# A planned mixture-of-experts kernel: TensorE's order taken from two lines instead of one

## The chip, the core and the metric

The kernel runs on one core of a Trainium2 chip. The core has a matrix engine (TensorE, PE in the profile), three engines for elementwise work (VectorE or DVE, ScalarE or ACT, GpSimd or POOL), a queue engine (SyncE or SP) and 16 DMA engines. SBUF is its working memory, PSUM the memory in eight banks that the matmuls write to. The metric is the device time of one execution in microseconds.

## What is computed

Sixteen sequences x of 256 tokens with 256 features pass through eight experts and one shared expert. All are gated feed-forward layers of width 1024, in float32:

```
g, u    = x @ Wg[e], x @ Wu[e]                  # e = 0..7, and Sg, Su
expert  = sum over e of p[b, e] * (silu(g) * u) @ Wd[e]
shared  = (silu(x @ Sg) * (x @ Su)) @ Sd
out     = x + (1 - s[b]) * expert + s[b] * shared
```

p and s are given for each sequence. The nine layers are treated alike: a coefficient made of p and s scales each hidden block.

## The kernel before, in words

The work is cut into 72 units: nine experts, two halves of the width, four groups of four sequences. Nearly every product of matrices is done in blocks with fewer multiplications than the plain way, at the price of sums of blocks.

For each unit, `unit_up` (line 622) makes the hidden blocks h. A *diagonal* step (`diagonal`, line 547) multiplies a plain block into bank D (two matmuls, the P part), ScalarE copies it out to pq, two more matmuls add the Q part to the same bank, and VectorE subtracts. There are four such steps, and only one bank D, so a step waits until the one before is consumed. An *off-diagonal* step (`offdiagonal`, line 590) does one matmul into a bank M (two of them). VectorE then adds M and a block s, which GpSimd made of pq, into a bank X (three of them): this add is called the seed. A pair of matmuls adds to that X. There are twelve such steps a unit. The results in D and X are consumed by ScalarE (silu, tile sg) for the gate half and by VectorE (multiplied by coefficient and sg, tile h) for the other half.

`unit_down` (line 709) multiplies h by Wd. VectorE and GpSimd first form four sums of blocks of h (the function `sum_`: three on VectorE, one on GpSimd, for each of two f). Then come seven products into banks dn (two of them), each of two matmuls with 512 columns. ScalarE copies a bank out to ev, and GpSimd starts a DMA that adds ev to running totals in DRAM. The down products of a unit are mixed into the up products of the next.

At the start, x is transposed on TensorE into banks dn (`make_raw`, line 447, and `make_xd`, line 409), and blocks of x and their sums are made (xd, xp), used, and kept in DRAM; later units load them. Unit 0 multiplies plain blocks. At the end, `finish` (line 819) loads the totals of a group, combines them on VectorE and GpSimd, transposes them on TensorE into banks dn and adds x. The last unit does without banks dn for its own product: `last_down` (line 884) writes it in eight steps of four matmuls to banks X and M.

What sets the order: all this is only entered into a list of operations (class `Plan`), each with an engine, a cost in us, a rank (the due place, 12 to a unit), what it depends on and the tiles it takes. `Plan.run` (line 77) then plays the list through on a clock of its own: each free engine takes the ready operation of lowest rank whose tiles are free, an operation's result can be used by another engine 0.25 us after its end (`HOP`), and transfers pass one after the other. The order in which operations are taken is the order in which the program's instructions are emitted. So every engine's order is fixed when the program is built; on the chip an engine runs it as written and waits by semaphores where an input is late.

The plan's costs are those of lines 222 to 233:

```
MM = 0.433                                    # matmul, 256 columns
TR = 0.16                                     # transpose
dve(n, stt) = (0.2 if stt else 0.12) + n * 0.00112
act(n) = 0.13 + n * 0.0009
pool(n) = 0.3 + n * 0.00215
```

The sums of h are charged 1.5 times `dve`. Tiles of one tag (banks dn, for one) are given out in the order of rank, whichever engine asks (`turn`).

TensorE is the exception to "lowest ready rank". Its operations stand in one list sorted by rank (`line`), and only the head of that list may be taken; if the head is not ready or its bank not free, TensorE waits in the plan.

Of the kernel before, what the change touches and what calls it, by code (L numbers as in the profile page):

```python
# [47 lines left out]
class Plan:  # L48
# [6 lines left out]

    HOP = 0.25
    KB = 0.0035

# [7 lines left out]
    def add(self, engine, length, rank, emit, deps=(), new=(), uses=(), lag=None, kb=None):  # L68
        lag = self.HOP if lag is None else lag
        op = Op(engine, length, lag, rank, emit, deps, list(new), list(uses))  # L70
        for b in [*op.new, *op.uses]:
            b.users += 1
        op.kb = kb
        self.ops.append(op)
        return op

    def run(self):
        free = self.slots
        ready = {}
        serial = {id(op): n for n, op in enumerate(self.ops)}  # L80
        for op in self.ops:
            ready.setdefault(op.engine, [])
        at = {id(op): 0.0 for op in self.ops}
        idle = {e: 0.0 for e in ready}
        events = []
        for op in self.ops:
            if not op.missing:
                heapq.heappush(events, (0.0, serial[id(op)], 0, op))
        order = []
        left = len(self.ops)  # L90
        line = sorted((op.rank, serial[id(op)]) for op in self.ops if op.engine == "PE")
        at_line = 0
        turn = {tag: deque() for tag in free}
        for op in sorted(self.ops, key=lambda op: (op.rank, serial[id(op)])):
            for b in op.new:
                turn[b.tag].append(b)
        now = passed = 0.0
        while left:
            while events and events[0][0] <= now + 1e-9:
                _, _, kind, op = heapq.heappop(events)  # L100
                if kind == 0:
                    heapq.heappush(ready[op.engine], (op.rank, serial[id(op)], op))
                elif kind == 1:
                    for b in [*op.new, *op.uses]:
                        b.users -= 1
                        if not b.users:
                            free[b.tag].append(b.tile)
            for e in ready:
                if idle[e] > now + 1e-9 or not ready[e]:
                    continue  # L110
                held, took = [], None
                while ready[e]:
                    item = heapq.heappop(ready[e])
                    if e == "PE" and item[:2] != line[at_line]:
                        held.append(item)
                        break
                    if all(free[b.tag] and turn[b.tag][0] is b for b in item[2].new) and all(
                        b.tile is not None for b in item[2].uses
                    ):
                        took = item[2]  # L120
                        for b in took.new:
                            b.tile = free[b.tag].popleft()
                            turn[b.tag].popleft()
                        break
                    held.append(item)
                for item in held:
                    heapq.heappush(ready[e], item)
                if took is None:
                    continue
                at_line += e == "PE"  # L130
                end = now + took.length
                idle[e] = end
                if took.kb:
                    passed = max(passed, end) + took.kb * self.KB
                    took.lag += passed - end
                order.append(took)
                left -= 1
                heapq.heappush(events, (end, serial[id(took)], 2, took))
                heapq.heappush(events, (end + took.lag, serial[id(took)], 1, took))
                for a in took.after:  # L140
                    a.missing -= 1
                    t = end if a.engine == e == "PE" else end + took.lag
                    at[id(a)] = max(at[id(a)], t)
                    if not a.missing:
                        heapq.heappush(events, (at[id(a)], serial[id(a)], 0, a))
            if left:
                if not events:
                    raise RuntimeError("the plan has come to a stop")
                now = max(now, events[0][0])
        return order  # L150
# [3 lines left out]
def kernel(  # L154
# [97 lines left out]
    def make_coef():  # L252
# [6 lines left out]
        )  # L259

    coef_op = add("DVE", 0.8, -2, make_coef)


# [5 lines left out]
    def load(rank, dst, src, kb, deps=(), new=(), uses=(), late=0, engine="SP"):  # L269
        queue = {"SP": nc.sync, "ACT": nc.scalar}[engine]  # L270
        return add(
            engine, 0.5, rank, lambda: queue.dma_start(dst(), src), deps, new, uses, lag=2.2 + late, kb=kb
        )

    def tt(engine, rank, o, a, b, op, n, deps, new=(), uses=(), slow=1.0):
        eng, length = (nc.vector, dve(n) * slow) if engine == "DVE" else (nc.gpsimd, pool(n))
        return add(engine, length, rank, lambda: eng.tensor_tensor(o(), a(), b(), op), deps, new, uses)  # L277
# [741 lines left out]
```

## Time and profile before

| | |
|---|---|
| time, median of 3 runs | 2534.58 us (2534.41 to 2534.78) |
| the profiled execution's own time | 2535.56 us |
| its span, first to last instruction | 2533.8 us |
| granted TensorE clock | 0.999 |
| HBM traffic | 167 GB/s over the span |

The profile is of one execution. Times are in us; a row of a group ends in the mean time of one instruction in ns. L277 and L282 are helpers of VectorE and GpSimd, L541 the one of all matmuls, so the tiles' names tell the operations apart: X<-M,s is the seed, h<-h,h a sum of h, dn<-h,wd a down product, dn<-ident a transpose, X<-xp,wp the pair of an off-diagonal step. A float32 matmul leaves two records. In an answer in the order of time, the first column is the start in the span, the second the time from the first start to the last end of the merged instructions, and a bracket at the end tells how long the engine was idle before and what released it. A wait is given as: engine and tile that waited, what it waited for, us in all, times, longest.

### The profile page before, as it was taken

The numbers are of one execution on the slowest core, as the hardware profiler recorded it, in microseconds if no ns is written. First come the engines' busy times: TensorE is split into PE (matmuls) and PEld (weight loads), VectorE is DVE, ScalarE is ACT, GpSimd is POOL, SyncE is SP. The second block draws the span as 40 slices with busy tenths as digits, with TensorE's granted clock in tenths as the row PEclk, the third lists the DMA queues.
The fourth block names the chain that finished last, engine by engine and source line by source line (L and its number), as shares of the span: only waits on it lengthen the run. The fifth ranks groups of instructions, "written<-read, shape, count | busy, mean of one in ns | idle before, by whom it ended". The sixth has DMA issues, their size and how long they took to land. (4 is left out here: it accounts for less than half of the span.)

```text
span 2533.8 us, 30307 instructions
## 1 busy us (share of the span) xinstructions
PE 2513.3 (99%) x9637; PEld 1817.8 (72%) x9637; DVE 1866.6 (74%) x3246; ACT 789.0 (31%) x1389; POOL 1722.7 (68%) x1652
## 2 busy tenths in 40 slices
PE   8999999999999999999999999999999999999998
PEld 5767777777777777777777777777777777777776
DVE  6796767677776768676767767677867777776687
ACT  3323333333333333333333332333332333333321
POOL 7686767676675767676766667586767676676664
PEclk9999999999999999999999999999999999999999
DMA  7545666665666566666666666566666565666566
GB/s 256 178 159 152 171 167 167 158 170 159 174 166 165 152 166 163 167 169 159 171 157 168 166 168 161 163 160 159 170 160 176 156 167 157 173 160 160 154 189 198
DMA packets 179667, 425.18 MB, mean 168 GB/s; under 512 B 15121, under 2 KB 84257, under 8 KB 170545
## 3 DMA queue, kind: packets, MB, share of 16 engines
q1 hardware_dynamic: 158224, 294.18, 34.8%
q0 software_dynamic: 20224, 128.53, 27.5%
q8 instruction: 76, 1.25, 0.2%
q14 instruction: 87, 0.70, 0.1%
q10 hardware_dynamic: 1056, 0.52, 0.1%
HBM read 276.90 MB, written 146.28 MB: 167 GB/s over the span
## 5 line engine op out<-in xcount | busy, mean ns | idle before, releaser
L277 POOL TENSOR_TENSOR s<-pq,pq 128x512 f32<-128x512 f32 x852 | 1145.3, 1373 | 495.8 <-DVE X L277 476.1
L541 PE MATMUL dn<-h,wd 128*128 128x512 f32 x1988 | 1015.1, 592 | 0.0
L541 PE MATMUL X<-xp,wp 128*128 128x256 f32 x3408 | 875.3, 379 | 6.1 <-DVE X L277 6.0
L277 DVE TENSOR_TENSOR X<-M,s 128x512 f32<-128x512 f32 x852 | 589.4, 694 | 392.3 <-PE M L541 255.5
L541 PEld LDWEIGHTS X<-xp,wp 128*128 128x128 f32 x3408 | 646.6, 190 | 218.2 <-issue 107.1
L541 PE MATMUL D<-xd,wb 128*128 128x256 f32 x2272 | 583.7, 379 | 2.7 <-ACT sg L639 2.2
L541 PEld LDWEIGHTS M<-xp,wp 128*128 128x128 f32 x1704 | 323.3, 190 | 347.1 <-issue 335.3
L282 DVE SCALAR_TENSOR_TENSOR h<-X,coef,sg 128x256 f32<-128x256 f32 x852 | 393.7, 479 | 211.4 <-PE X L541 158.9
L541 PE MATMUL M<-xp,wp 128*128 128x256 f32 x1704 | 506.9, 379 | 0.5 <-DVE X L277 0.5
L761 ACT COPY ev<-dn 128x512 f32<-128x512 f32 x490 | 287.8, 587 | 681.1 <-PE dn L541 681.1
L541 PEld LDWEIGHTS D<-xd,wb 128*128 128x128 f32 x2272 | 431.0, 190 | 66.2 <-ACT sg L639 4.6
L277 DVE TENSOR_TENSOR h<-h,h 128x512 f32<-128x512 f32 x426 | 453.5, 1090 | 0.0
L541 PEld LDWEIGHTS dn<-h,wd 128*128 128x128 f32 x1988 | 377.4, 190 | 51.2
L568 ACT COPY pq<-D 128x512 f32<-128x512 f32 x284 | 166.5, 586 | 418.1 <-PE D L541 389.2
L639 ACT ACTIVATE sg<-X 128x512 f32<-128x512 f32 x434 | 258.4, 595 | 111.9 <-PE X L541 104.6
L776 POOL DMA_DIRECT2D total<-ev x132 | 116.6, 884 | 208.2 <-ACT ev L761 199.3
L277 DVE TENSOR_TENSOR pq<-D,pq 128x256 f32<-128x256 f32 x568 | 222.5, 416 | 29.5 <-PE D L541 29.3
L639 ACT ACTIVATE sg<-D 128x512 f32<-128x512 f32 x142 | 84.8, 597 | 483.5 <-DVE pq L277 483.5
L277 POOL TENSOR_TENSOR h<-h,h 128x512 f32<-128x512 f32 x142 | 199.5, 1405 | 49.3 <-PE dn L541 31.0
L277 POOL TENSOR_TENSOR wp<-wb 128x128 f32<-128x128 f32 x216 | 139.4, 681 | 0.0
L282 DVE SCALAR_TENSOR_TENSOR h<-D,coef,sg 128x256 f32<-128x256 f32 x284 | 134.9, 475 | 0.0
L282 DVE SCALAR_TENSOR_TENSOR wp<-wb,wp 128x256 f32<-128x256 f32 x102 | 89.9, 882 | 0.0
(73 smaller groups left out, 482.6 us busy)
## 6 DMA issues: line engine op xcount, KB each, us to landing
xp<-keep_p SPq DMA_DIRECT2D x408, 384.0 KB, 4.0
total<-ev POOLq DMA_DIRECT2D x70, 1024.0 KB, 7.9
xd<-keep_d SPq DMA_DIRECT2D x136, 512.0 KB, 3.5
total<-ev POOLq DMA_DIRECT2D x70, 768.0 KB, 6.8
wb<-in_L_cond_Wg_dram SPq DMA_DIRECT2D x32, 256.0 KB, 5.2
wb<-in_L_cond_Wu_dram SPq DMA_DIRECT2D x32, 256.0 KB, 5.2
wd<-in_L_cond_Wd_dram SPq DMA_DIRECT2D x64, 128.0 KB, 4.0
keep_p<-xp SPq DMA_DIRECT2D x18, 384.0 KB, 4.0
```

Of the source, the lines that this page charges most:

```text
L277: return add(engine, length, rank, lambda: eng.tensor_tensor(o(), a(), b(), op), deps, new, uses)
L282: lambda: nc.vector.scalar_tensor_tensor(o(), a(), c() if callable(c) else c, b(), ALU.mult, op),
L541: lambda: nc.tensor.matmul(o(), w(), mv(), start=start, stop=stop, skip_group_check=onto),
L568: lambda: nc.scalar.copy(p_[:, 2 - 2 * a : 4 - 2 * a, :], bank[:, :, :]), ps,
L639: lambda: nc.scalar.activation(b[:, :, :], bank[:, :, :], AF.Silu), deps, [b], [bank],
L761: lambda ev=ev, at=at, bank=bank: nc.scalar.copy(ev[:, at, :], bank.tile.rearrange("p a t -> p (a t)")),
L776: nc.gpsimd.dma_start(total[g][part], ev[:, 0:k, :], accum_op=ALU.add)
```

## The change

Each TensorE operation gets a stream: 1 if it takes or uses a tile with the tag dn (down products and all transposes), 0 otherwise (everything in banks D, M and X, the last unit's down product among them). Each stream has its own list sorted by rank. TensorE, when free in the plan, goes through its ready operations by rank; one that isn't the head of its own list is set aside and the search goes on, where before it ended. It takes the first head whose tiles are free. So a down product may pass a waiting up product, or the other way, while the order within each list stays as it was.

```diff
@@ add
         op.kb = kb
+        op.stream = None
+        if engine == "PE":
+            op.stream = int("dn" in [b.tag for b in [*op.new, *op.uses]])
         self.ops.append(op)
@@ run
-        line = sorted((op.rank, serial[id(op)]) for op in self.ops if op.engine == "PE")
-        at_line = 0
+        lines = {k: deque(sorted((op.rank, serial[id(op)]) for op in self.ops if op.stream == k)) for k in (0, 1)}
...
-                    if e == "PE" and item[:2] != line[at_line]:
+                    if e == "PE" and item[:2] != lines[item[2].stream][0]:
                         held.append(item)
-                        break
+                        continue
...
-                at_line += e == "PE"
+                if e == "PE":
+                    lines[took.stream].popleft()
```

## Prediction

> **What bounds the kernel now.** I read the totals of the page first, then the stages, then what TensorE (PE) waits for, then single places in the order of time.
>
> ```profile
> span 2533.8 us, 30307 instructions
> ...
> PE 2513.3 (99%) x9637; PEld 1817.8 (72%) x9637; DVE 1866.6 (74%) x3246; ACT 789.0 (31%) x1389; POOL 1722.7 (68%) x1652
> ```
>
> PE is busy all but 20.5 us; no other engine is near that. The busy time by stages shows where those 20.5 us lie (first column the stage, then its length, then each engine's busy time):
>
> ```profile
> 0.00:60.00 60.00, 53.51 (x180) 29.87 (x181) 38.66 (x74) 21.39 (x46) 44.82 (x66) 0.97 0.82 264
> 60.00:200.00 140.00, 134.91 (x520) 96.40 (x519) 120.63 (x200) 44.82 (x83) 100.60 (x101) 1.00 0.47 167
> 200.00:2400.00 2200.00, 2199.78 (x8426) 1600.38 (x8425) 1604.04 (x2803) 695.89 (x1214) 1503.91 (x1428) 1.00 0.63 164
> 2400.00:2500.00 100.00, 98.25 (x390) 70.54 (x389) 80.98 (x136) 25.72 (x45) 67.58 (x54) 1.00 0.77 221
> 2500.00:2534.00 34.00, 26.81 (x128) 20.57 (x126) 22.26 (x36) 1.20 (x2) 5.82 (x5) 1.00 0.33 109
> ```
>
> In 2200 us in the middle PE is idle for 0.22 us. An order of PE's instructions can't save anything there; it can only lose. Idle are 6.5 us up to 60 us, 5.1 up to 200, 1.8 from 2400 to 2500 and 7.2 after that, the last 3.4 of them after PE's work, when the last add and store run out. What ended PE's waits:
>
> ```profile
> PE X L541 <- DVE X L277: 6.0, 7, 1.4
> PE dn L862 <- DVE xd L277: 2.9, 3, 1.9
> PE D L541 <- ACT sg L639: 2.2, 3, 1.0
> ```
>
> So the largest item is a pair of X matmuls (the other line, in the new words) that waits for VectorE's seed of its bank, the next a transpose (the down line) that waits for a dn bank. In both cases the head of PE's one queue waits, and behind it stands work of the other kind. That is what the change is aimed at.
>
> **The change, part by part.** It adds and removes no instruction: the same 9637 matmuls, copies and DMAs. It alters the order in which the plan emits PE's instructions, and, as a consequence of times in the plan, the order on DVE, ACT, POOL and SP (the transfers of these queues go with them).
>
> *Ceiling of the gain.* The idle marked in the order of time, where the other line had work, is 0.70 us before the transposes at 96.26, before X pairs 1.36 (138.19), 1.27 (168.55), 0.62 (175.47), 1.00 (182.76), 1.01 (2430.67), 0.55 (2488.41) and 0.19 (2491.89), before transposes at the end 1.88 (2515.25), 0.70 (2517.47) and 0.35 (2524.11): 9.6 us. In the first 60 us the D pairs wait 0.92, 0.50 and 1.02 us and an M matmul 0.55; the down line holds only transposes there (0.44 us for four records), the last of them already done at 36.4, so I count 0.4 for the first wait and nothing for the others. The ceiling is 10.0 us. A down product takes 0.86 us from start to start, so one or two fill each gap. Time filled early is kept, since PE is full afterwards and DVE (1604 of 2200 us) is not; at the end the next thing late is the load of x for the last adds, which held DVE for 0.4 us up to 2525.6, 4.8 us before the last add ends at 2530.4. It doesn't take back more than that.
>
> The Trainium skill (Perfetto Trace Analysis, Identifying the Most-Contended Engine) says that the matmul row's occupancy is no measure of the distance to PE's limit. I therefore also added up start-to-start distances over the normal ones (0.43 us for 256 columns, 0.86 for 512, two records each): they exceed them by 22.2 us in all, 6.4 of it after 2400. Against 20.5 by busy time the ceiling would be some 1 us higher, and the middle stays full. The reading stands.
>
> *How much of it the plan can take.* "Ready" is decided when the program is written, by the plan's own clock; on the chip PE still runs one fixed order. A wait is filled only if the plan also sees it. The plan charges DVE 0.12 + 512 x 0.00112 = 0.69 us for an add of 512 columns, 1.5 times that (1.04) for a sum of h. Now look at two of the gaps:
>
> ```profile
> 161.94 3.26 DVE L277 TENSOR_TENSOR h<-h,h 128x512 f32<-128x512 f32 x1
> ```
>
> ```profile
> 166.25 1.02 PE L541 MATMUL dn<-h,wd 128*128 128x512 f32 x2
> ...
> 167.81 0.68 DVE L277 TENSOR_TENSOR X<-M,s 128x512 f32<-128x512 f32 x1
> ...
> 168.41 0.68 DVE L277 TENSOR_TENSOR h<-h,h 128x512 f32<-128x512 f32 x1
> 168.55 0.70 PE L541 MATMUL X<-xp,wp 128*128 128x256 f32 x2 [1.27 <-DVE X L277]
> ```
>
> ```profile
> 2512.95 1.63 DVE L277 TENSOR_TENSOR ev<-ev 128x512 f32<-128x512 f32 x1
> ...
> 2514.51 0.68 DVE L277 TENSOR_TENSOR xd<-dn,xd 128x512 f32<-128x512 f32 x1
> ...
> 2515.25 0.66 PE L862 MATMUL dn<-ident,wb 128*128 128x128 f32 x4 [1.88 <-DVE xd L277]
> ```
>
> The same form of sum takes 0.68 us in one place and 3.26 in another; that one is 2.2 us over the plan's 1.04, more than the 1.27 us wait that follows. Before 2515.25, three adds on DVE took 1.44, 1.43 and 1.63 us where the plan has 0.69: 2.4 us over, more than the 1.88. By the same count, a sum of 2.12 before 96.26 is 1.1 over (wait 0.70), an xp sum of 3.51 instead of 0.41 precedes 138.19 with no pause of DVE in between (3.1 over, wait 1.36), two sums of 3.04 together precede 175.47 (1.0 over, wait 0.62), and adds of 1.58 and 1.70 precede 2430.67 (1.9 over, wait 1.01). In these, 6.8 of the 9.6 us, DVE in the plan is early enough that PE doesn't wait there, and nothing is swapped. The waits at 2488 and 2491 have no such cause (two sums of 1.89 against 2.08 planned), those at 182.76, 2517.47 and 2524.11 only in part.
>
> Here the skill speaks against the change. SBUF — State Buffer, Who interferes with whom: a DVE instruction with two inputs in SBUF and a GpSimd instruction that reads SBUF exclude each other, and the later one waits for the whole of the other. The groups agree in kind: the seed has one input in PSUM, the sum of h two in SBUF, at equal size:
>
> ```profile
> L277 DVE TENSOR_TENSOR X<-M,s 128x512 f32<-128x512 f32 x852 | 589.4, 694 | 392.3 <-PE M L541 255.5
> ...
> L277 DVE TENSOR_TENSOR h<-h,h 128x512 f32<-128x512 f32 x426 | 453.5, 1090 | 0.0
> ```
>
> By the mean row (1090 ns) the plan's 1.04 is right and its clock ought to see most gaps: up to 10.0 us gained. By the rule, the length of a sum depends on what POOL happens to do, the gaps come from single long ones, and a plan with a mean can't see them: 0 to 3.2 us (10.0 less 6.8). The single rows, 0.68 and 3.26, side with the rule. I take half of it, 1.6 us.
>
> *What can be lost.* Where the plan sees a wait that the chip doesn't have, a down product of 0.86 us passes an X or D pair. From 200 to 2400 us I took, for all 766 X pairs, the time from the seed's end to the pair's start: median 2.8 us, smallest 0.32; where PE really waited it is 0.05. Passing one is therefore free nearly everywhere: the pair starts 0.86 later, PE has worked meanwhile, and DVE has 27% idle to absorb it. In 14 places, one for each change of weights (138 us apart), it is only 0.32 to 0.36; the plan adds 0.25 for the hand-over, so its own margin is about 0.1 us and a swap there is possible. Below nothing: a swap of work that is ready on the chip costs 0. Above: the advanced product's sum of h is late on the chip, 2.12 - 1.04 = 1.1 us. I take 0, since the margin is positive in every one of them. DVE's and POOL's order shifts a little with the plan; that moves single collisions either way, which I set at ±2 us.
>
> **Rivals.**
> - *All gaps filled* (chance 0.12): the plan is late enough in the same places. 2534.6 - 9 = 2525.6. For it: the waits are the right kind, head of line with other work behind. Against: DVE's long sums.
> - *The fixed order gains a wait in the middle* (0.07), slower than before: at each of the 17 changes of weights the plan lets a down product pass and its sum is late on the chip. 17 x 0.5 (half of 1.1) = 8.5 us: 2543.1. It decides from 0.3 us a change on. For it: margins of 0.1 us, sums of up to 3.26. Against: no such wait now, and PE needs that product late enough that most sums are long done.
> - *The plan never differs* (0.11): PE's head is always ready on the plan's clock, the program is the same, 2534.6.
>
> **How the numbers follow.** The profiled execution took 2535.56 us, its span is 2533.8; what is taken off the span is taken off the time, and I set it against the median of 2534.58, 0.98 lower. Likeliest (0.70): 2534.6 - 1.6 = 2533.0, own range 2529.5 to 2537. A measurement can tell 0.2%, 5.1 us: faster means under 2529.5, slower over 2539.6. Faster: the first rival and a tail of the likeliest, 0.12 + 0.03. Slower: 0.07. The range takes in the likeliest case, the unchanged program and the near part of both others: 2528 to 2538.5, some 0.17 left out.
>
> **What would show it.** Right: PE idle of about 19 us instead of 20.5; the 1.27 before an X pair near 168 and the 1.88 near 2515 still there in kind; from 200 to 2400 still under 1 us. Wrong: these waits gone, with down products in their places (first rival), or waits of PE on dn with DVE h or POOL h as releaser in the middle (second). If PE's order is the same throughout, the third. My weakest step is that I infer the plan's waits from its costs and the trace's durations.

## The result, and the profile after

2527.62 us (median of 9 runs) against 2534.58: 7.0 us less, ratio 0.9973 with a 95% interval of 0.9963 to 0.9983. The prediction was 2533.0, within 0.2% of no change, in a range of 2528 to 2538.5. The time lies just under the range, between the likeliest case and the rival that I had given 0.12 (all gaps filled, 2525.6), 2.0 us from that rival.

The page's head for the changed kernel, beside 2513.3 us of PE in a span of 2533.8 before:

```profile
span 2525.9 us, 30304 instructions
...
PE 2512.4 (99%) x9637; PEld 1817.6 (72%) x9637; DVE 1850.4 (73%) x3246; ACT 788.1 (31%) x1389; POOL 1718.6 (68%) x1652
```

The number of matmuls is the same, and so, nearly, is their busy time. What went is idle time. The stages of the changed kernel (stage, length, busy time of PE, PEld, DVE, ACT, POOL):

```profile
0.00:60.00 60.00, 56.62 (x194) 32.47 (x195) 41.09 (x76) 22.08 (x48) 46.25 (x68) 1.00 0.83 271
60.00:200.00 140.00, 137.27 (x530) 98.18 (x529) 127.10 (x205) 44.88 (x83) 104.94 (x104) 1.00 0.50 174
200.00:2400.00 2200.00, 2199.80 (x8425) 1600.33 (x8424) 1582.79 (x2806) 696.00 (x1215) 1497.01 (x1427) 1.00 0.63 164
2400.00:2500.00 100.00, 98.45 (x388) 70.16 (x387) 82.25 (x136) 24.55 (x43) 65.36 (x53) 1.00 0.73 211
2500.00:2534.00 34.00, 20.31 (x106) 16.52 (x104) 17.23 (x27) 0.60 (x1) 5.07 (x4) 0.97 0.33 109
```

Read the first two columns and take PE's busy time off the length: up to 60 us PE idles for 3.4 us in place of 6.5; from 60 to 200 for 2.7 in place of 5.1; in the middle for 0.2 as before; from 2400 to 2500 for 1.55 in place of 1.75; and from 2500 to the end of the span (2525.9) for 5.6 in place of 7.0 (the stage of before ends at 2533.8, so 7.0 and not the 7.2 of the prediction). So the gain lies in the first 200 us and at the end. The two profiled executions differ by 7.9 us, the medians by 7.0. Part of the rest is in the first 15 us, where the order of PE is the same in both: the execution of before had a granted clock of 0.89 there, this one 1.00, and its first transposes waited 1.64 us for x against 0.29.

PE's waits, X pairs on the seed first (6.0 us before), then transposes on a dn bank (2.9), then D (2.2):

```profile
PE X L545 <- DVE X L281: 3.5, 7, 0.7
PE dn L866 <- DVE xd L281: 1.7, 2, 1.4
...
PE D L545 <- ACT sg L643: 0.8, 2, 0.6
...
PE dn L545 <- DVE ev L281: 0.4, 1, 0.4
```

The last row is new: a down product that now stands ahead of an X pair waits at 2485.66 for the add on VectorE that empties its bank. It is not the mechanism of the slower rival, a product whose sum of h is late; no wait of that kind is on the list. In the order of time (start, length, PE's instructions), this is what shortened waits look like:

```profile
27.07 1.04 PE L427 MATMUL dn<-ident,h 128*128 128x128 f32 x8
28.70 1.13 PE L545 MATMUL D<-xd,wb 128*128 128x256 f32 x4 [0.59 <-ACT sg L643]
...
34.84 1.88 PE L545 MATMUL X<-pq,wb 128*128 128x512 f32 x4
36.56 1.02 PE L545 MATMUL dn<-h,wd 128*128 128x512 f32 x2
37.42 1.03 PE L545 MATMUL D<-xd,wb 128*128 128x256 f32 x4
```

At 27.07 eight records of transposes stand before the D that waits (0.59 us, 0.92 before); before the change they came after it, at 30.39 and 32.54. At 36.56 stands the first down product of unit 0, which before ran at 56.57, and the D behind it, which waited 0.50 us at 38.82, doesn't wait any more. Of the 2116 records of the down line, 160 stand earlier against the other line than before, and 24 later. The later ones are two matmuls of down products and one block's transposes in the first 100 us, and transposes at the end.

### The profile page after: what moved, and what is told of

Read it like the earlier page. It is cut to its first block, busy times and chain, and to the rows that moved or that the text cites. A ratio compares the mean times of both kernels' runs of the same rounds, so it can differ in the third digit from the quotient of the medians.

```text
span 2525.9 us, 30304 instructions
## 1 busy us (share of the span) xinstructions
PE 2512.4 (99%) x9637; PEld 1817.6 (72%) x9637; DVE 1850.4 (73%) x3246; ACT 788.1 (31%) x1389; POOL 1718.6 (68%) x1652
## 5 line engine op out<-in xcount | busy, mean ns | idle before, releaser
L281 POOL TENSOR_TENSOR wp<-wp,wb 128x256 f32<-128x256 f32 x108 | 81.8, 764 | 1.3
```

## The experiments

The times of before beside them are those of the same chip, 2534.75 to 2534.83 us.

**Where in the run the gain arises.** Three kernels allow passing only in a part of the run. The condition is on the rank of the lower of the two heads, `low`:

```diff
+                    if e == "PE" and item[:2] != (low := min(q[0] for q in lines.values() if q)) and not (low[0] < 60):
+                        held.append(item)
+                        continue
```

with `60 <= low[0] < 830` and `low[0] >= 830` in the two others.

> One list as before, except while the lower of the two heads has a rank under 60 (about the first 190 us): there the two lists. My theory (the plan's own clock has PE waiting in the first units where the chip waits, and ready work of the other list fills it): PE idle up to 200 us falls from 11.6 to about 6, the rest stays as before; 2529.3 us, 5.3 of the 7.0. Rival 1 (the gain comes from the 40 or so places in the middle that were also swapped, through fewer collisions of DVE and POOL): 2534 us. Rival 2 (much of the gain is in the first 15 us, a matter of chance between executions): 2532 to 2533 us.

Measured: 2529.56 us, ratio 0.9979 (0.9971 to 0.9987), 5.3 us less. PE's idle from 60 to 200 us is 2.76 us, from 15 to 60 us 0.52 in place of 2.99. Up to 200 us that makes 7.2 us in place of 11.6, not the 6 that I expected, since 3.9 of it lie in the first 15 us of the profiled execution, where nothing was reordered. The time is as my theory had it; the rivals fall.

> Two lists only while the lower head's rank is from 60 to 830 (about 190 to 2420 us), one list else. My theory: PE has no idle time there (0.22 us in 2200), so the swaps cost and bring nothing: 2534.6 us within 0.4. Rival 1: 2529 us or less. The rival of the prediction (a swapped down product that is late on the chip at a change of weights): 2537 us or more, with PE waiting on dn products.

Measured: 2534.67 us, ratio 1.0 (0.9992 to 1.0008). In this kernel 49 down products stand one X pair earlier, and its row for the middle is

```profile
200.00:2400.00 2200.00, 2199.79 (x8425) 1600.40 (x8424) 1583.63 (x2803) 695.80 (x1214) 1501.07 (x1428) 1.00 0.62 164
```

DVE is busy for 20 us less than before (1583.6 against 1604.0) and it buys nothing: PE is full either way. PE waits for 0.2 us there in all, so the slower rival of the prediction falls as well.

> Two lists only from rank 830 on (the last 110 us). My theory: the up products that pass the waiting transposes at the end, and down products that pass X pairs at 2430 and 2488, give 1.6 us: 2533.0. Rival: the end is set by the last loads, adds and stores, and nothing comes of it: 2534.6.

Measured: 2532.69 us, ratio 0.9991 (0.9983 to 0.9999), 2.1 us less, 0.5 more than expected. The three parts add up to 7.6 us against 7.0 for the whole.

**Which line passes.** Both lists, but in the condition above `item[2].stream == 1` in place of the rank: only down products and transposes may pass.

> Two lists, but only the list with down products and transposes may pass; a waiting down product or transpose holds up the others as before. My theory: nearly all of the gain in the first 200 us is of this direction (of the places there one, the transposes at 96 us with 0.70 of idle, is of the other), and the end, where up products pass transposes, is lost again: 2529.8 us. Rival (the gain needs both directions, since one line's lead must be given back by the other): 2532 us or more.

Measured: 2530.5 us, ratio 0.9983 (0.9976 to 0.999), 4.3 us less: 0.7 us short of my number, and 1.5 from the rival's. Idle after 2500 us is 6.95 us, as before the change: without up products passing transposes the end gains nothing. From 60 to 200 us it is 3.47 in place of 2.73, the wait at 96 us.

**How much comes from the first 55 us.** The condition with `low[0] < 13`.

> Two lists only while the lower head's rank is under 13 (about the first 55 us), one list after. In the prediction I counted 0.4 us for these, since I took the down list to hold nothing but transposes there. My theory now: a transpose at 27 us and the first down product of unit 0 at 36 us fill two waits, and the waits of D at 46 and of M at 54 shrink since all before them is earlier; idle from 15 to 60 us falls from 3.0 to under 1.2, and the time to 2532.6. Rival (the fall of idle in that stage needs the swaps after rank 13 too): 2534 us.

Measured: 2532.47 us, ratio 0.999 (0.9984 to 0.9997), 2.3 us less. Idle from 15 to 60 us falls from 2.99 to 0.74 us, all the rest stays (5.09 us from 60 to 200). One wait of 0.71 us is left in that stage, the M matmul's; it was 0.55 before and did not shrink as I had expected.

**What makes the plan see a wait.** Which waits are filled depends on the plan's clock, and that on its costs. First lower costs, with one list as the control and with two:

```diff
-    HOP = 0.25
+    HOP = 0.05
...
                     deps, [out_] if new else [], [x_, y_] if new else [x_, y_] if out_ in (x_, y_) else [x_, y_, out_],
-                    1.5,
+                    1.0,
```

> One list as before, with lower costs in the plan: hand-over 0.05 us in place of 0.25 and sums of h at 0.69 in place of 1.04. PE's order can't change by it; only DVE, ACT, POOL and SP are ordered otherwise. A control for the next run: 2534.6 within 2 us by every theory.

Measured: 2532.68 us, ratio 0.9991 (0.9983 to 0.9999): 2.1 us less with PE in the same order, by the order of the other engines alone.

> Two lists with the same low costs. With these the plan's clock has PE waiting in the first 60 us, hardly at all from 60 to 200 us, and for about 1 us at the end. My theory (only a wait that the plan sees is filled, and the plan sees those from 60 to 200 us because it charges 0.25 for a hand-over and 1.04 for every sum of h): the waits from 60 to 200 us, 5 us before and 2.7 after, stay as they are in the control, and the gain over the control is 3 to 4 us instead of 7. Rival (the costs don't matter, any list scheduling that is free to pass finds these places): 6 us or more over the control.

Measured: 2529.59 us, ratio 0.998 (0.9973 to 0.9988), 3.1 us under its control in place of 7.0. From 60 to 200 us the stage row is

```profile
60.00:200.00 140.00, 137.32 (x531) 98.27 (x530) 117.58 (x203) 45.51 (x84) 107.35 (x107) 1.00 0.51 177
```

which is 2.7 us idle against 3.7 in the control: 1.0 us gained there, where the old costs gain 2.4. "Stay as they are" was too strong; that lower costs halve the gain held. Then only the hand-over lowered:

> Two lists, only the plan's hand-over lowered from 0.25 to 0.05 us, what the chip shows; sums of h keep 1.04. My theory: part of the loss of the run with low costs is from this, part from the sums; this one lies between the two lists with low costs (2529.6) and with the old ones (2527.6): 2528.5. Rival (the sums alone decide which waits the plan sees): 2527.6.

Measured: 2526.16 us, ratio 0.9965 (0.9952 to 0.9977). Both expectations miss: it is 1.5 us better than with the old costs, and idle from 60 to 200 us is 1.2 us. So it is not the generous hand-over that makes the plan see the waits. Between this kernel and the one with low costs only the charge for sums of h differs, 1.04 against 0.69, and 3.4 us of time. A control with one list and only the short hand-over was not run, so how much of these differences comes from the order of the other engines is not known.

Then higher costs, again with the control. Three kinds of DVE instructions with both inputs in SBUF get about what the trace shows:

```diff
-                op = stt(rank + 1, r, x_, float(t), r, ALU.add, P, [u, v], uses=[b])
+                op = stt(rank + 1, r, x_, float(t), r, ALU.add, P, [u, v], uses=[b], more=0.6)
...
-            [bi, bj], [buf] if new else [], src if new else [buf, *src],
+            [bi, bj], [buf] if new else [], src if new else [buf, *src], 2.3,
...
-                uses=list({id(m[q][1]): m[q][1] for q in (o, a, c)}.values()),
+                uses=list({id(m[q][1]): m[q][1] for q in (o, a, c)}.values()), slow=1.5,
```

> One list, with the costs of three kinds of DVE instructions with both inputs in SBUF raised to what the trace shows: sums of x 0.94 in place of 0.41, combinations at the end 1.04 in place of 0.69, the base sum of weights 0.94 in place of 0.34. PE's order is unchanged. A control: 2534.6 within 2 us.

Measured: 2535.09 us, ratio 1.0 (0.9992 to 1.0008): by the order of the other engines alone these costs bring nothing.

> Two lists with these high costs, so that the plan sees more of the chip's waits (some 6 us from 60 to 200 us and 7 at the end in place of 3.6 and 4). My theory: 1 to 3 us less than the two lists with the old costs, 2525 to 2526.5. Rival (what is left are single long instructions of DVE that no mean cost can place): 2527.6 within 0.7.

Measured: 2522.14 us, ratio 0.995 (0.9938 to 0.9963): 12.7 us less than before, 13.0 under its control and 5.5 under the change itself, more than I expected. The stages:

```profile
0.00:60.00 60.00, 56.73 (x197) 32.74 (x198) 41.94 (x78) 22.32 (x49) 46.98 (x68) 1.00 0.83 271
60.00:200.00 140.00, 139.56 (x541) 100.71 (x540) 126.43 (x207) 46.44 (x86) 106.06 (x106) 1.00 0.50 177
...
2500.00:2534.00 34.00, 16.53 (x92) 14.15 (x90) 12.55 (x22) 0.00 (x0) 2.54 (x2) 0.94 0.33 109
```

From 60 to 200 us PE idles for 0.44 us; the control, with the same costs and one list, for 5.45. The rival, that single long instructions can't be placed by a mean cost, falls. After 2500 us (the span ends at 2520.3) 3.8 us are left, all of them after PE's last matmul, for the last add and store.

> Two lists with the high costs of the run before and, on top, 1.39 us for a sum of h on DVE in place of 1.04. If a cost above the mean is a useful margin against single long sums, 2521 us or less. If a cost is best at its mean (the trace's 1.09 to 1.12), the plan sees waits that the chip doesn't have, and the time rises to 2523 or more.

Measured: 2521.93 us, ratio 0.9948 (0.9935 to 0.9962): neither of the two, 0.2 us from the run without it. The charge may lie a quarter above the mean (1.39 against 1.12 in the run without it); it decides nothing here.

> Two lists, the high costs of DVE's instructions with two inputs in SBUF, and the hand-over of 0.05 us. The short hand-over gave 1.5 us with the old costs (2526.2 against 2527.6). If the two add: 2520.6. Rival (what the short hand-over gained was in gaps that the high costs fill already, and a plan with less margin meets single long sums): 2522 or more. It can't go below about 2518: PE's busy time of 2512.5, 1.2 before its first instruction, 3.4 of store after its last, and 1.8 between span and time.

Measured: 2521.08 us, ratio 0.9948 (0.9934 to 0.9961), the lowest of the study, 13.7 us under before. It lies between the two expectations; of the 1.5 us that the short hand-over gave with the old costs, 1.1 remain. PE's waits in this kernel:

```profile
PE X L269 <- DVE zero L242: 1.2, 1, 1.2
PE M L545 <- DMA wb<-in_L_cond_Wu_dram: 0.9, 1, 0.9
PE X L545 <- ACT pq L470: 0.7, 1, 0.7
PE dn L427 <- DVE xd L286: 0.4, 1, 0.4
PE X L545 <- DVE X L281: 0.3, 1, 0.3
```

The first three lie in the first 15 us, where the order of PE is that of before. Of X pairs on the seed, 6.0 us before, 0.3 are left.

## Why the prediction was wrong, step by step

*Ceiling of the gain, 10.0 us.* Right in kind, too low. In the first 60 us PE waits four times, 3.0 us together, and I counted 0.4, because I took the down line to hold only transposes there. The kernel with passing in the first 55 us alone gained 2.3. The first matmul of a unit's down product takes one block of h only, and unit 0's was ready at 36 us, 20 us before its place in the one list. With these four waits the ceiling is 12.6 us, and the two lists with the high costs gained 13.0 over their control.

*How much of it the plan can take.* This is the step that failed. I wrote that in 6.8 of the 9.6 us "DVE in the plan is early enough that PE doesn't wait there, and nothing is swapped", and put the gain there at nothing. In the changed kernel the same six operations wait for 0, 0.49, 0.68, 0.47, 0.54 and 1.44 us in place of 0.70, 1.36, 1.27, 0.62, 1.01 and 1.88: 3.6 in place of 6.8, a gain of 3.2 us. The X pair at 138 before the change, and the same pair after it:

```profile
135.81 1.03 PE L541 MATMUL D<-xd,wb 128*128 128x256 f32 x4
138.19 1.13 PE L541 MATMUL X<-xp,wp 128*128 128x256 f32 x4 [1.36 <-DVE X L277]
139.16 1.02 PE L541 MATMUL dn<-h,wd 128*128 128x512 f32 x2
```

```profile
132.66 1.02 PE L545 MATMUL dn<-h,wd 128*128 128x512 f32 x2
134.17 1.13 PE L545 MATMUL X<-xp,wp 128*128 128x256 f32 x4 [0.49 <-DVE X L281]
```

The plan's own waits, which I had only inferred, can be had by playing `Plan.run` of the kernel before through and noting when PE stands still. At the six places they are 0.57, 0.05, 0, 0.31, 0 and 0.43 us. So the inference that the plan sees these waits shorter than the chip was right; what I made of it was wrong, in two ways. First, a wait needn't be seen in its full length: at 138, where the plan of one list waits for 0.05 us, a whole down product goes ahead with two, and the chip's wait falls by 0.87 us. Second, the plan's waits are not those of the one list any more once the first are filled, since PE comes earlier to the next pair: at 2430 the plan of one list has none, and with two lists a down product goes ahead all the same. One of the six is luck: at 168 no work was put ahead of the X pair, and the sum of h before it happened to take 1.76 us in place of 3.26.

The excess of one long instruction over its cost was the wrong measure for this. The plan's 1.04 us is close to a mean, and the trace of before has 180 of the 426 sums at under 0.75 us beside 68 of over 2 us. Over a stretch they balance in part: from 60 to 200 us PE waits 3.6 us in the plan and 5.1 on the chip, though not at the same places. The run with a charge of 0.69 instead of 1.04 points the same way: with its low costs the plan of one list doesn't wait at all from 60 to 200 us, and it is 3.4 us slower than the run that differs from it in this charge alone.

The other 2.8 of the 9.6 us, which I had left as seen in part, gave less than I allowed for. All five went, but six others of 0.2 to 0.6 us, 2.3 together, came up elsewhere.

*The row or the rule.* I set the mean row (1090 ns: the plan sees most gaps, up to 10 us) against the rule of the Trainium skill (SBUF — State Buffer, Who interferes with whom) that the later of two instructions waits for the whole of the other, sided with the rule, and took 1.6 us, a half for which I had no measurement. The trace of before bears out that the long sums are waits for GpSimd (last section), and goes beyond the rule: of the 68 sums of over 2 us all overlap two GpSimd instructions or three, not one. What I drew from it was wrong: that a plan with a mean cost can't place such gaps. One list against two with the raised mean costs, 2535.09 against 2522.14, shows that it can.

*What can be lost.* Right in the result: the middle alone gave 2534.67 us with 49 passings. Not right in the working: I looked for at most 14 places where the plan might let a down product pass. Its clock has PE waiting for 13 us between 200 and 2400 us, in 48 waits of 0.22 or 0.39 us, where the chip has 0.2 us in all, so many more pairs were passed. It cost nothing, as I wrote, since the pairs have room: the smallest distance from a seed's end to its X pair between 200 and 2400 us, 0.32 before, is 0.49 after, and the 14 pairs at 0.32 to 0.36 are now at 1.2.

*The end.* Right in that it is not bound by the loads and stores: 2.1 us for the last part alone. Of the 7.0 us of idle time after 2500 us before the change, 3.8 and not 3.4 lie after PE's last matmul, out of reach. The 1.88 us wait of the transposes near 2515 is there in kind, as I wrote, shortened to 1.44 at 2509:

```profile
2506.55 1.03 PE L545 MATMUL X<-xd,h 128*128 128x256 f32 x4
2509.02 0.66 PE L866 MATMUL dn<-ident,wb 128*128 128x128 f32 x4 [1.44 <-DVE xd L281]
```

Two matmuls of the last product (four records of X) now go ahead of the waiting transposes; then the plan thinks the transposes ready, the chip's DVE is late, and PE waits with further matmuls behind. Here my argument held: the old cost of the final combinations was too low for the plan to see all of it.

*What stays open.* Why lower costs with one list gain 2.1 us though PE's order is the same, and why a short hand-over gains 1.5 with two, was not taken apart; both change the order on DVE, ACT and POOL. One trait goes with it: in the four kernels planned with a hand-over of 0.05 us the longest sum of h takes 2.5 us and the mean is 1.02 to 1.05, in the ten others 3.7 and 1.08 to 1.12.

## What to carry to other kernels

Where one engine is full for nearly the whole run, look at its head and tail by stages and ask at each wait what stands behind it that is independent; a second list that may pass cost nothing here where the engine is full. A schedule fixed at build time does this better with honest costs: measured means, also for instructions whose times spread widely, were worth another 5.5 us, a charge a quarter above the mean did no harm, and one a third below the plan's 1.04 went with a loss. Don't judge such a plan by one long instruction, and don't infer its waits: its clock can be played through and read before anything runs.

## What the runs showed of the hardware that I had not expected

A VectorE sum of 512 columns with both inputs in SBUF (h<-h,h) took from 0.67 to 3.7 us in one execution, with a mean of 1.09 before and after. The trace of before tells where the time goes. All 246 sums of 0.75 us or more end 0.55 or 0.56 us after the end of a GpSimd instruction; of the 180 shorter ones 158 overlap none. The seed, with one input in PSUM, took 0.68 to 0.70 us in all 852 cases, though 529 of them overlap a GpSimd instruction. And a waiting sum can be passed over: of the 68 sums of over 2 us, 67 sat through a GpSimd instruction that began after the sum's recorded start. Here is the sum of 3.26 us that the prediction shows, beside GpSimd's instructions:

```profile
161.46 1.28 POOL L277 TENSOR_TENSOR s<-pq,pq 128x512 f32<-128x512 f32 x1
161.94 3.26 DVE L277 TENSOR_TENSOR h<-h,h 128x512 f32<-128x512 f32 x1
162.69 0.73 POOL L277 TENSOR_TENSOR xp<-xd,xp 128x256 f32<-128x256 f32 x1
163.37 1.27 POOL L277 TENSOR_TENSOR s<-pq,pq 128x512 f32<-128x512 f32 x1
```

The sum starts while the first of three runs, and ends at 165.20, 0.56 us after the third. Its length was set by three GpSimd instructions without a pause between them. The mean moved little with the order of the engines, 1.02 to 1.12 over all fourteen kernels, so a mean could be given for a cost.
